# Linear-attention sums taken per head from projected values, and one more band of filter taps on TensorE

## The chip, the cores and the metric

The kernel runs on one core of one Trainium2 chip. The metric is the device time of one execution in microseconds (us). Three runs of the kernel before gave a median of 3430.04 us (3429.32 to 3433.61). One further execution was recorded by the hardware profiler.

Engines are named as in the profile: PE is TensorE's matrix multiplication and PEld its weight loads, DVE is VectorE, ACT is ScalarE, POOL is GpSimd, SP is the engine that issues most DMAs.

## What is computed

The input is x of 8 images, 384 channels, 64 x 64 pixels (4096 tokens each), in float32. Two residual layers follow one another, each on a group-normalised input:

```
# layer 0: linear attention, 6 heads of 64 channels
q = elu(rope(Wq x + bq) / 8) + 1
k = elu(rope(Wk x + bk)) + 1
v = Wv x + bv
kv    = einsum('bhnd,bhne->bhde', k, v)       # sum over 4096 tokens
k_sum = k.sum(tokens)
out   = einsum('bhnd,bhde->bhne', q, kv) / (q . k_sum + 1e-6)
x = x + Wfc out + bfc
# layer 1: 1x1 conv, FFT filter on 8x8 blocks, 3x3 depthwise conv, gate
t = irfft2(rfft2(blocks(w_in x)) * fft_filter)
t = depthwise_conv3x3(t, w_dw)                # 9 taps per channel
x = x + w_out (gelu(t[:192]) * t[192:])
```

## The kernel before

**Tiling.** The 384 channels are three tiles of 128 partitions. The 4096 tokens of an image are eight bands of 512 (8 rows of 64 pixels). `nb` is 8 images, `b` counts images, `j` bands, `m` and `t` channel tiles, `i` the four groups of 128 tokens in a band.

**Stages.** After a start-up that forms the keys of image 0, two stages alternate for each image.

- The *attention stage* of image b (`queries`, L823): per band a query projection (`q_project`, L527, PSUM tiles pq), rotation and elu on DVE and ACT, a normaliser (`q_normalise`, L565, pn, and `q_spread`, L589, prb), the output projection (`project_out`, L606, pf), which adds into x. Its end holds the norm chain of layer 1, a row of small dependent steps on PE, DVE and ACT. The key projections of bands 0 and 1 of the next image are put between these steps as filling.
- The *filter stage* of image b (layer 1): per band `expand_filter` (L624 pi, L638 pd, product tf on DVE at L646), `back_transform` (L659 pb, copied by ACT into one of two ring buffers, L669 to L675), `first_taps` (ACT) and `taps` (DVE, L720, eight scalar_tensor_tensor per channel tile), the gate (L726 to L731), and `contract` (L747 and L758, pw). The keys of image b+1 are formed here as well: an iterator `fill` is advanced between the pieces of each band.

**Keys and values before.** For all images, a band's keys are projected with tokens on the partitions (`k_project`, L432, pk; the bias is added by DVE at L435 into kc; the rotation is L415, L423, L439, the elu L337 to L339). The x of the same band is transposed by PE in twelve 128 x 128 pieces (`turn_tokens`, L398, px) and copied by ACT (L399) into xk, with a column of ones from POOL (L391). Then `kx_accumulate` (L447) sums keys times x, not keys times values: for each of the four token groups three matmuls of 128 key channels by 385 columns, into three PSUM banks `acc` that are held from band 0 of the filter stage to the end of the key sums. At j = 0 and 1 `fill` is the accumulation of bands 0 and 1. At j = 2 it is the projection of band 2, and from j = 3 on the projection of band j and the accumulation of band j-1.

`kv_finish` (L457) turns these sums into what the attention needs. It copies acc to kx (ACT L464, DVE L462), turns the key sums into a row (L468 pr), transposes kx (nine pieces, L485 pt, copied at L486), multiplies by the value weights per head (L494 pv, 24 matmuls of 64 columns in halves of the array and their bias row), copies the result into kvt_bd (DVE L502) and multiplies by wfc (L509 pm) into mt. Twelve POOL copies (L476) spread the key sums into ks_bd, which pn reads. The first three parts of `kv_finish` alternate with the three column blocks of `q_project(b, 1)`.

**Order.** Each engine works through a fixed order made when the program is built. It follows the program text, except that an instruction whose inputs are not due yet is passed by later ones. PSUM is eight banks, one tile each, that rotate; a matmul waits until a bank has been read out. `work` has nine slots for large SBUF tiles (tag w).

At the start of each attention stage three things of the filter stage are still open: the contraction of band 6 (`before_last`, called after `q_project(b, 0)`), the taps and gate of band 7 (`gate`, called in the loop at j = 0, 24 instructions of L720), and the contraction of band 7 (`output`, called at j = 2).

In the last image there are no next keys. Its filter stage runs `expand_filter`, `back_transform`, `first_taps`, `contract` and `taps` band by band. In bands 6 and 7 the third channel tile's nine taps are matmuls with diagonal matrices instead (`array_taps`, L694, ptap): `on_array` says which. In band 6 six of the nine are issued by `first_taps(b, 6)` and three by `taps(b, 6)`, since the last row comes from band 7.

Of the kernel before, what the change touches and what calls it, by code (L numbers as in the profile page):

```python
# [16 lines left out]
CT = 3  # L17
# [100 lines left out]
def conv_blocks_kernel(ctx: ExitStack, tc: tile.TileContext, a: dict, out: bass.AP, nb: int):  # L118
# [253 lines left out]
    def v_bias(b, params):  # L372

        p_ = ps_tile(f"pbv_{b}")
        nc.tensor.matmul(p_[:1, :C], params[2], group_w["wv"], start=True, stop=True)
        t = small.tile([1, C], F32, tag="krest", name=f"vbias_{b}", bufs=1)
        nc.vector.tensor_add(t, p_[:1, :C], bv)
        return t


    transposed = {}
# [19 lines left out]
    def k_project(b, j, wks, bias, kf):  # L401

        tk = qp.tile([P, 2, 4, 2, QC], F32, tag="turn", name=f"tk_{b}_{j}")
        nc.sync.dma_start(tk, a["tk"][:, j])
        xk = transposed.pop((b, j), None)
        early = xk is not None
        if not early:
            xk = xk_tile(b, j)
        kc = w_tile([P, 4, C], f"kc_{b}_{j}")
        ks = w_tile([P, 4, C], f"ks_{b}_{j}")  # L410
        def turn_keys(r):

            k, to = (t[:, r].rearrange("p i (g c) -> p (i g) c", g=2) for t in (kc, ks))
            cos, sin = (tk[:, i, r].rearrange("p i g f -> p (i g) f") for i in range(2))
            nc.vector.tensor_mul(  # L415
                to.rearrange("p g (s f two) -> p g s f two", s=2, two=2),
                k.rearrange("p g (s c) -> p g s c", s=2)[:, :, ::-1, :].rearrange(
                    "p g s (f two) -> p g s f two", two=2
                ),
                sin.rearrange("p g (s f) -> p g s f", s=2).unsqueeze(4).to_broadcast([P, 4, 2, QC // 2, 2]),  # L420
            )
            pairs = k.rearrange("p g (f two) -> p g f two", two=2)
            nc.vector.tensor_mul(pairs, pairs, cos.unsqueeze(3).to_broadcast([P, 4, QC, 2]))  # L423

        for i in range(4):

            def tokens(t):
                return xt[b, j][:, t, i * P : (i + 1) * P]

            pk = ps_tile(f"pk_{b}_{j}_{i}")  # L430
            for t in range(CT):
                nc.tensor.matmul(pk[:, :C], tokens(t), wks[:, t, :], start=(t == 0), stop=(t == CT - 1))  # L432
            if not early:
                turn_tokens(b, j, i, xk)
            nc.vector.tensor_add(kc[:, i, :], pk[:, :C], bias)  # L435
            if i % 2:
                turn_keys(slice(i - 1, i + 1))
            yield
        nc.vector.tensor_add(kc, kc, ks)  # L439
        elu_plus_one(kc, ks)  # L440
        kf[j] = kc, xk

    def kx_accumulate(b, j, kf, xk, acc):

        for i in range(4):
            for m in range(CT):
                nc.tensor.matmul(  # L447
                    acc[m][:, : C + 1],
                    kf[:, i, m * P : (m + 1) * P],
                    xk[:, i, :],  # L450
                    start=(j == 0 and i == 0),
                    stop=(j == NBAND - 1 and i == 3),
                )
            yield

    def kv_finish(b, acc, params, vb, wv, wfc, done):

        rs = params[0]
        kx = w_tile([P, CT, C + 1], f"kx_{b}")
        for m in range(CT):  # L460
            if m == 1:
                nc.vector.tensor_copy(kx[:, m, :], acc[m][:, : C + 1])  # L462
            else:
                nc.scalar.copy(kx[:, m, :], acc[m][:, : C + 1])  # L464
        row = small.tile([1, C], F32, tag="ksrow", name=f"ksrow_{b}", bufs=1)
        pr = ps_tile(f"pr_{b}")
        for m in range(CT):
            nc.tensor.matmul(  # L468
                pr[:1, m * P : (m + 1) * P], kx[:, m, C : C + 1], ident, start=True, stop=True
            )  # L470
        nc.scalar.copy(row, pr[:1, :C])
        for c0, at, n in QRUNS:

            for s in range(0, n, 32):
                h, c, q = (c0 + s) // HD, c0 + s, at + s
                nc.gpsimd.tensor_copy(  # L476
                    ks_bd[q % P : q % P + 32, q // P, h : h + 2 * NH + 1 : NH],
                    kx[c % P : c % P + 32, c // P, C : C + 1].to_broadcast([32, 3]),
                )
        yield  # L480
        xks = w_tile([P, CT, C], f"xks_{b}")
        for t in range(CT):
# [7 lines left out]
        for m in range(CT):  # L490
            for t in range(-1, CT):
                for h in range(2):
                    head = slice(m * P + h * HD, m * P + (h + 1) * HD)
                    nc.tensor.matmul(  # L494
                        pv[halves[h], m * HD : (m + 1) * HD],
                        vb[:, head] if t < 0 else wv[:, t, head],
                        row[:, head] if t < 0 else xks[:, t, head],
                        start=(t < 0),
                        stop=(t == CT - 1),
                    )  # L500
# [2 lines left out]
                kvt_bd[halves[h], :, halves[h]], pv[halves[h], :C // 2].rearrange("p (m k) -> p m k", m=CT)  # L503
            )
        yield
        mt = small.tile([P, CT, C], F32, tag="mt", name=f"mt_{b}", bufs=1)
        for t in range(CT):
            pm = ps_tile(f"pm_{b}_{t}")
            nc.tensor.matmul(pm[:, :C], kvt_bd[:, t, :], wfc[:, t, :], start=True, stop=True)  # L509
            for i, (c, at, n) in enumerate(QPIECES):  # L510
                if c // P == t:
                    dst, src = mt[at % P : at % P + n, at // P, :], pm[c % P : c % P + n, :C]
                    if i % 2:
                        nc.vector.tensor_copy(dst, src)
                    else:
                        nc.scalar.copy(dst, src)
        done.append(mt)


    def q_project(b, j, wqs, bias, q):  # L520
# [159 lines left out]

    def on_array(b, j):

        return b == nb - 1 and j >= NBAND - 2

    def make_diagonals():
        t = small.tile([P, CT, C], F32, tag="wk", name="diagonals", bufs=1).rearrange("p t c -> p (t c)")
# [24 lines left out]
    def taps(b, j):  # L711

        t, acc = ring[j % 2], dw[b, j]
        if on_array(b, j) and j < NBAND - 1:
            array_taps(b, j, range(6, 9))
        for m in range(CT - on_array(b, j)):
            for k in range(1, 9):
                src = t[:, m, k // 3 : k // 3 + 8, k % 3 : k % 3 + W]
                wd = w_dw[:, m, k : k + 1]
                nc.vector.scalar_tensor_tensor(acc[:, m], src, wd, acc[:, m], ALU.mult, ALU.add)  # L720
# [84 lines left out]
    class Keys:  # L805
# [5 lines left out]
                self.params, self.wk, self.bias = prepared  # L811
                self.kf = {}

        def project(self, j):
            if self.live and j < NBAND:
                yield from k_project(self.b, j, self.wk, self.bias, self.kf)

        def accumulate(self, j):
            if self.live and 0 <= j < NBAND:
                if j == 0:  # L820
                    self.acc = [ps_tile(f"acc_{self.b}_{m}") for m in range(CT)]
                yield from kx_accumulate(self.b, j, *self.kf.pop(j), self.acc)

        def prepare(self, j):

# [4 lines left out]
                scale_weight(self.wq, self.params, scale)  # L830
                self.qbias = q_bias(self.b, self.params)
            if self.live and j == NBAND:
                self.wv, self.wfc = (load_weight(self.b, n, k_runs) for n in ("wv", "wfc"))
                if self.b == 0:
                    sum_weight(self.wv, "wv")
                self.vbias = v_bias(self.b, self.params)

    def queries(b, keys, before_last, gate, output):


        params, wq, qbias, wv, wfc, vbias = keys.params, keys.wq, keys.qbias, keys.wv, keys.wfc, keys.vbias
        q, done = {}, []
        run(q_project(b, 0, wq, qbias, q))
        before_last()
        run(keys.accumulate(NBAND - 1))
        finish = kv_finish(b, keys.acc, params, vbias, wv, wfc, done)
        for _ in zip(q_project(b, 1, wq, qbias, q), finish):
            pass
        prepared = []
# [44 lines left out]
    keys = Keys(0, prepared)  # L894
    run(keys.project(0))

    bv = const_tile([1, C], "bv", a["bv"].unsqueeze(0), nc.sync)
    bq = const.tile([P, CT], F32, tag="bq", name="bq")
    for c0, at, n in QRUNS:

# [47 lines left out]
    for b in range(nb):  # L948
        prepared = queries(b, keys, before_last, gate, output)
        keys = Keys(b + 1, prepared)  # L950
        params = []
        chain, more = norm_chain(b, 1, params), chain_of(keys.project(0), keys.project(1))
        last = b == nb - 1
        if last:

# [7 lines left out]
        run(more)  # L963
        if last:
            break
        first_sums = chain_of(keys.accumulate(0), keys.accumulate(1))
        for j in range(NBAND):
            fill = chain_of(keys.project(j), keys.accumulate(j - 1 if j > 2 else NBAND)) if j > 1 else first_sums
            tf = []
            h = normalised(b, j, params, (8, 8), "f") if j else ahead  # L970
            store_x(b, j)
            if 1 <= j < NBAND - 1:
                load_x(b + 1, j + 1)
            layer1 = expand_filter(b, j, h, tf)
            next(layer1)
            next(fill)
            run(layer1)
            next(fill)
            next(fill)
            back_transform(b, j, tf[0])  # L980
            first_taps(b, j)
            next(fill)
            if j > 1:
                contract(b, j - 2)
            if j > 0:
                run(fill)
            keys.prepare(j)
            if j > 0:
                depthwise_gate(b, j - 1)
            stream_stats(b + 2, j)  # L990
# [15 lines left out]
    for j in range(NBAND):  # L1006
# [4 lines left out]
        if j < NBAND - 1:  # L1011
            h = normalised(b, j + 1, params, (8, 8), "f")
        back_transform(b, j, tf[0])
        first_taps(b, j)
        if j >= 2:
            contract(b, j - 2)
# [48 lines left out]
```

## Time and profile before

| | us |
|---|---|
| median of 3 runs | 3430.04 |
| the profiled execution | 3431.62 |
| its span, first to last instruction | 3428.8 |
| granted TensorE clock, mean | 0.994 |
| filter stage of image 1 (751.3 to 988.0) | 236.7 |
| attention stage of image 2 (988.0 to 1170.8) | 182.8 |
| filter stage of image 7 (3249.7 to 3428.8) | 179.1 |

A stage is counted here from the first record of pq (L527) or of pi (L624) of an image. The stages of images 1 to 5 repeat to 0.1 us. Between the profiled span and the execution's own time lie 2.8 us.

How to read it: a row of groups ends with busy time and mean duration of one, then the idle time of its engine before it and what ended that. A matmul in float32 here has two records; a transpose has one. Records overlap, since the array is a pipeline: what one more costs is the distance between starts, not the duration of one.

### The profile page before, as it was taken

How to read it: one execution, taken by the hardware profiler on the slowest of the kernel's cores; microseconds unless marked ns; L12 is line 12 of the kernel's file. 1: busy time of each engine (PE TensorE's matmuls, PEld its weight loads, DVE VectorE, ACT ScalarE, POOL GpSimd, SP SyncE). 2: the span in 40 equal slices, each digit the busy share in tenths (PEclk: the TensorE clock that was granted, in tenths of full speed). 3: DMA queues.
4: the chain of work that ended last, by engine and by line, in shares of the span. 5: the costliest groups of instructions: out<-in, count | busy, mean ns of one | idle time of the engine just before them, and what ended most of it. 6: DMA issues, size and time to landing. Idle time of an engine off the chain costs nothing.

```text
span 3428.8 us, 50015 instructions
## 1 busy us (share of the span) xinstructions
PE 3337.2 (97%) x19760; PEld 1866.2 (54%) x19760; DVE 2801.2 (82%) x4396; ACT 1958.6 (57%) x3869; POOL 140.2 (4%) x247
## 2 busy tenths in 40 slices
PE   8999999999999999999999999999999999999988
PEld 5545555455654556545565455654556445564454
DVE  6586888869898698986989869897698967989598
ACT  4445666456655567545665557555576455554553
POOL 0000001000010000100001000010000000000000
PEclk9999999999999999999999999999999999999999
DMA  6323234333243333442343423334243331333113
GB/s 219 113 90 108 70 107 97 124 118 80 78 108 122 109 84 88 106 127 93 84 105 99 126 93 93 100 97 124 84 111 89 102 121 47 83 85 96 61 25 51
DMA packets 149328, 335.60 MB, mean 98 GB/s; under 512 B 27125, under 2 KB 38246, under 8 KB 140902
## 3 DMA queue, kind: packets, MB, share of 16 engines
q1 hardware_dynamic: 123702, 282.65, 24.8%
q0 software_dynamic: 25200, 49.55, 9.2%
q8 instruction: 155, 2.54, 0.3%
q14 instruction: 79, 0.65, 0.1%
q10 hardware_dynamic: 192, 0.21, 0.0%
HBM read 232.51 MB, written 99.88 MB: 97 GB/s over the span
## 4 chain that ended last, share of the span: by engine, by line
PE 64%; DVE 28%; ACT 5%; issue 2%; DMA 0%; SPq 0%; DVEq 0%; ACTq 0%
DVE dw L720 17%; PE pf L606 15%; PE pq L527 13%; PE acc L447 10%; PE pk L432 8%; PE pi L624 6%; PE pw L747 3%; PE pb L659 2%; DVE kc L439 2%; PE pd L638 2%; PE pw L758 1%; DVE kc L339 1%; DVE kc L435 1%; ACT ring L669 1%; PE pn L565 1%
## 5 line engine op out<-in xcount | busy, mean ns | idle before, releaser
L720 DVE SCALAR_TENSOR_TENSOR dw<-ring,w_dw,dw 128x512 f32<-128x512 f32 x1520 | 1061.4, 744 | 179.3 <-ACT ring L675 137.7
L432 PE MATMUL pk<-wk,x 128*128 128x384 f32 x1536 | 547.2, 495 | 8.7 <-DVE kc L435 8.7
L527 PE MATMUL pq<-x,wq 128*128 128x512 f32 x1152 | 520.8, 599 | 4.0 <-ACT qs L554 3.9
L606 PE MATMUL pf<-qc,mt 128*128 128x512 f32 x1152 | 513.6, 599 | 0.0
L624 PE MATMUL pi<-w_in,hf 128*128 128x384 f32 x1536 | 510.8, 489 | 2.1 <-ACT hf L332 1.3
L447 PE MATMUL acc<-xk,kc 128*128 128x385 f32 x1488 | 504.0, 492 | 0.0
L624 PEld LDWEIGHTS pi<-w_in,hf 128*128 128x128 f32 x1536 | 290.4, 191 | 204.9 <-issue 5.1
L447 PEld LDWEIGHTS acc<-xk,kc 128*128 128x128 f32 x1488 | 276.4, 190 | 204.5 <-issue 22.8
L432 PEld LDWEIGHTS pk<-wk,x 128*128 128x128 f32 x1536 | 278.1, 190 | 197.5 <-issue 22.8
L527 PEld LDWEIGHTS pq<-x,wq 128*128 128x128 f32 x1152 | 211.9, 190 | 255.1 <-issue 240.7
L606 PEld LDWEIGHTS pf<-qc,mt 128*128 128x128 f32 x1152 | 213.0, 190 | 250.0 <-issue 232.8
L399 ACT COPY xk<-px 128x384 f32<-128x384 f32 x248 | 118.1, 486 | 324.5 <-PE px L398 324.5
L631 ACT COPY ht<-pi 128x384 f32<-128x384 f32 x256 | 120.2, 479 | 235.7 <-PE pi L624 235.1
L610 DVE SCALAR_TENSOR_TENSOR x<-pf,bfc,x 128x512 f32<-128x512 f32 x192 | 140.9, 742 | 106.8 <-PE pf L606 106.2
L435 DVE TENSOR_TENSOR kc<-pk,kbias 128x384 f32<-128x384 f32 x256 | 141.2, 552 | 86.9 <-PE pk L432 85.6
L747 PE MATMUL pw<-gated,w_out 128*128 128x256 f32 x768 | 183.9, 386 | 5.7 <-DVE kc L435 5.6
L337 ACT ACTIVATE qs<-qc 128x1536 f32<-128x1536 f32 x64 | 95.0, 1484 | 158.0 <-DVE qc L556 148.0
L554 ACT ACTIVATE qs<-pq,qbias 64x512 f32<-64x512 f32 x128 | 87.3, 682 | 168.1 <-DVE qc L540 167.2
L179 ACT ACTIVATE differences<-x,shift 128x512 f32<-128x512 f32 x168 | 119.9, 714 | 77.1 <-DVE x L610 77.1
L777 POOL DMA_DIRECT2D out_dram<-y x63 | 80.7, 1281 | 2019.2 <-ACT y L772 1938.7
L669 ACT COPY ring<-pb 128x256 f32<-128x256 f32 x384 | 115.8, 406 | 81.3 <-PE pb L659 81.3
L747 PEld LDWEIGHTS pw<-gated,w_out 128*128 128x128 f32 x768 | 141.8, 192 | 33.6 <-DVE kc L435 11.3
(157 smaller groups left out, 4354.3 us busy)
## 6 DMA issues: line engine op xcount, KB each, us to landing
tq<-in_tq SPq DMA_DIRECT2D x64, 1024.0 KB, 4.8
x<-in_x SPq DMA_DIRECT2D x64, 768.0 KB, 6.3
tk<-in_tk SPq DMA_DIRECT2D x64, 768.0 KB, 4.5
out_dram<-x SPq DMA_DIRECT2D x63, 768.0 KB, 3.3
out_dram<-y POOLq DMA_DIRECT2D x63, 768.0 KB, 7.9
xs<-in_x SPq DMA_DIRECT2D x56, 768.0 KB, 5.8
wk<-in_wk SPq DMA_DIRECT2D x8, 576.0 KB, 3.9
wv<-in_wv SPq DMA_DIRECT2D x8, 576.0 KB, 3.7
```

The costliest lines, as they stand in the source:

```text
L179: nc.scalar.activation(out[:, m, :], x_[:, m, :], AF.Identity, bias=shift[:, m : m + 1], accum_out=of_m[0])
L432: nc.tensor.matmul(pk[:, :C], tokens(t), wks[:, t, :], start=(t == 0), stop=(t == CT - 1))
L435: nc.vector.tensor_add(kc[:, i, :], pk[:, :C], bias)
L447: nc.tensor.matmul(acc[m][:, : C + 1], kf[:, i, m * P : (m + 1) * P], xk[:, i, :], start=(j == 0 and i == 0), stop=(j == NBAND - 1 and i = ...
L527: nc.tensor.matmul(p_, wqs[:, t, m * P : (m + 1) * P], xt[b, j][:, t, :], start=(t == 0), stop=(t == CT - 1),)
L606: nc.tensor.matmul(p_, mt[:, t, m * P : (m + 1) * P], q[:, t, :], start=(t == 0), stop=(t == CT - 1))
L610: nc.vector.scalar_tensor_tensor(xm, p_, bfc[:, m : m + 1], xm, ALU.add, ALU.add)
L624: nc.tensor.matmul(p_[:, :C], h[:, t, i * P : (i + 1) * P], w_in[:, t, :], start=(t == 0), stop=(t == CT - 1),)
L631: nc.scalar.copy(ht[:, i, :], p_[:, :C])
L669: nc.scalar.copy(rows[:, u], ps[u][:, m - m0].rearrange("p s i (r c) -> p r s i c", r=8))
L720: nc.vector.scalar_tensor_tensor(acc[:, m], src, wd, acc[:, m], ALU.mult, ALU.add)
L747: nc.tensor.matmul(p_[h][:, m - m0, :], w_out[:, 0, m * P : (m + 1) * P], gated[:, h * HT : (h + 1) * HT], start=(m == m0), stop=False,)
```

## The change

For image 0 nothing changes but names. For images 1 to 7:

- The transposes of x (px) and their copies go. `v_project` projects the values with tokens on the partitions (twelve matmuls of 384 columns a band), and ACT copies them into a tile with 65 columns a head, the last one ones.
- `kv_accumulate` multiplies keys by values per head: 24 matmuls a band, 64 key channels by 65 columns, even heads into the upper and odd heads into the lower half of one PSUM bank.
- `kv_finish_heads` replaces `kv_finish`: one copy, six small DVE instructions that add the value bias times the key sums, three transposes.
- The value weights are loaded and scaled with the next image's keys (`load_values`), into the buffer of mt.
- `fill` has more pieces: the values of band 0 and 1 now come in the filter stage at j = 0 and 1, those of later bands after each piece of keys.

In the last image the third tile's taps of band 3 go to TensorE too, and the last three of a band's matmuls are issued ahead of the next `first_taps`.

```diff
     def k_project(b, j, wks, bias, kf):
...
-        early = xk is not None
-        if not early:
+        early = b or xk is not None
+        if b:
+            xk = w_tile([P, 4, NH, HD + 1], f"v_{b}_{j}")
+            nc.gpsimd.memset(xk[:, :, :, HD:], 1.0)
+        elif not early:
             xk = xk_tile(b, j)
...
+    def v_project(b, j, wvs, v):
+        for i in range(4):
+            pv = ps_tile(f"pv_{b}_{j}_{i}")
+            for t in range(CT):
+                nc.tensor.matmul(pv[:, :C], xt[b, j][:, t, i * P : (i + 1) * P], wvs[:, t, :],
+                    start=(t == 0), stop=(t == CT - 1))
+            nc.scalar.copy(v[:, i, :, :HD], pv[:, :C].rearrange("p (h d) -> p h d", h=NH))
+            yield
+
+    def kv_accumulate(b, j, kf, v, acc):
+        for i in range(4):
+            for head in range(NH):
+                m, h = head // 2, head % 2
+                nc.tensor.matmul(
+                    acc[halves[h], m * (HD + 1) : (m + 1) * (HD + 1)],
+                    kf[:, i, head * HD : (head + 1) * HD],
+                    v[:, i, head, :],
+                    start=(j == 0 and i == 0 and m == 0),
+                    stop=(j == NBAND - 1 and i == 3 and m == CT - 1))
+            yield
...
+    def kv_finish_heads(b, acc, vb, wfc, done):
+        kx = w_tile([P, CT, HD + 1], f"kx_{b}")
+        nc.scalar.copy(kx, acc[:, : CT * (HD + 1)].rearrange("p (m d) -> p m d", m=CT))
+        key_sums(kx, HD)
+        for m in range(CT):
+            for h in range(2):
+                head = 2 * m + h
+                nc.vector.scalar_tensor_tensor(kvt_bd[halves[h], m, halves[h]],
+                    vb[halves[h], head * HD : (head + 1) * HD], kx[halves[h], m, HD : HD + 1],
+                    kx[halves[h], m, :HD], ALU.mult, ALU.add)
+        yield
+        kvt = w_tile([P, CT, P], f"kvt_{b}")
+        pt = ps_tile(f"pt_{b}")
+        for m in range(CT):
+            nc.tensor.transpose(pt[:, m * P : (m + 1) * P], kvt_bd[:, m, :], ident)
+        nc.scalar.copy(kvt, pt[:, : CT * P].rearrange("p (m k) -> p m k", m=CT))
+        yield
+        yield
+        fold(b, kvt, wfc, done)
...
-        return b == nb - 1 and j >= NBAND - 2
+        return b == nb - 1 and j in (3, NBAND - 2, NBAND - 1)
...
-        if on_array(b, j) and j < NBAND - 1:
-            array_taps(b, j, range(6, 9))
...
+        def load_values(self):
+            if self.live:
+                self.wv = small.tile([P, CT, C], F32, tag="mt", name=f"wv_{self.b}", bufs=1)
+                nc.sync.dma_start(self.wv, w_in_dram["wv"])
+                scale_weight(self.wv, self.params)
+            yield from ()
...
-        chain, more = norm_chain(b, 1, params), chain_of(keys.project(0), keys.project(1))
+        chain, more = norm_chain(b, 1, params), chain_of(keys.project_k(0), keys.load_values(), keys.project_k(1))
...
-        first_sums = chain_of(keys.accumulate(0), keys.accumulate(1))
+        first_values = keys.project_v(0)
+        next(first_values, None)
         for j in range(NBAND):
-            fill = chain_of(keys.project(j), keys.accumulate(j - 1 if j > 2 else NBAND)) if j > 1 else first_sums
+            if j < 2:
+                fill = chain_of(keys.project_v(j) if j else first_values, keys.accumulate(j))
+            else:
+                fill = chain_of(keys.project(j), keys.accumulate(j - 1 if j > 2 else NBAND))
...
         back_transform(b, j, tf[0])
+        if j and on_array(b, j - 1):
+            array_taps(b, j - 1, range(6, 9))
         first_taps(b, j)
```

`fold` and `key_sums` are the old ends of `kv_finish` under names of their own. The value bias becomes a tile of 128 equal rows.

## The prediction

> **What bounds the kernel now.** I read the page's busy shares first, then the groups by form, then a table of stretches through one round of stages (filter stage of image 1, attention stage of image 2), then PE's and DVE's timelines where that table shows DVE full.
>
> ```profile
> PE 3337.2 (97%) x19760; PEld 1866.2 (54%) x19760; DVE 2801.2 (82%) x4396; ACT 1958.6 (57%) x3869; POOL 140.2 (4%) x247
> ...
> 751.30:789.30 38.00, 37.95 (x321) 22.06 (x322) 23.73 (x36) 21.83 (x47) 0.37 (x2) 1.00 0.33 104
> 789.30:816.10 26.80, 25.04 (x198) 15.62 (x196) 26.12 (x42) 17.28 (x39) 0.00 (x0) 1.00 0.11 31
> 816.10:852.50 36.40, 33.61 (x223) 20.49 (x222) 36.16 (x52) 29.21 (x57) 2.79 (x4) 1.00 0.50 132
> ...
> 974.70:1019.90 45.20, 45.20 (x201) 25.69 (x199) 42.75 (x65) 27.62 (x46) 8.39 (x14) 1.00 0.45 103
> 1019.90:1071.60 51.70, 51.14 (x268) 24.93 (x265) 47.81 (x79) 25.27 (x42) 0.00 (x0) 1.00 0.32 111
> 1071.60:1149.50 77.90, 77.90 (x334) 34.69 (x333) 54.51 (x93) 43.66 (x96) 1.48 (x3) 1.00 0.39 119
> ```
>
> The columns after the length are PE, PEld, DVE, ACT, POOL, then clock and DMA. PE is full nearly everywhere, so PE work is the first price. But DVE is full too in two places: bands 2 and 3 of the filter stage (26.12 of 26.8, 36.16 of 36.4), where PE stalls, and the stretch from 974.7, when the ring of band 7 is ready, to 1071.6, the end of the contraction of band 7 (90.6 of 96.9).
>
> **PE's work per image.** Starts, not durations, are the price.
>
> ```profile
> L432 PE MATMUL pk<-wk,x 128*128 128x384 f32 x1536 | 547.2, 495 | 8.7 <-DVE kc L435 8.7
> L447 PE MATMUL acc<-xk,kc 128*128 128x385 f32 x1488 | 504.0, 492 | 0.0
> L398 PE MATMUL px<-groups,x 128*128 128x128 f32 x768 | 124.4, 277 | 12.1 <-DMA x<-in_x 6.5 <-ACT ht L631 4.7 <-ACT ring L399 0.4
> L494 PE MATMUL pv<-xks,wv 128*64 128x64 f32 x288 | 13.6, 230 | 0.0
> ```
>
> ```profile
> 1007.87 2.74 PE L527 MATMUL pq<-x,wq 128*128 128x512 f32 x6
> 1010.54 0.82 PE L468 MATMUL pr<-groups,kx 128*1 128x128 f32 x6
> 1011.29 2.84 PE L527 MATMUL pq<-x,wq 128*128 128x512 f32 x6
> 1013.97 1.15 PE L485 MATMUL pt<-groups,kx 128*128 128x128 f32 x9
> 1014.96 2.74 PE L527 MATMUL pq<-x,wq 128*128 128x512 f32 x6
> 1017.63 0.33 PE L494 MATMUL pv<-ksrow,vbias 1*64 1x64 f32 x4
> 1017.89 0.57 PE L494 MATMUL pv<-xks,wv 128*64 128x64 f32 x12
> ```
>
> Median distances of starts in the trace: pk 322 ns, acc 323, px 109 (pt too: 0.99 us for nine above).
> - Removed: px 96 x 0.109 = 10.5 us; acc 192 x 0.323 = 62.0; in the finish pr 0.75, pt 0.99, pv 2.27 (1017.63 to pn at 1019.90) = 4.0. Sum 76.5.
> - Added: values 192 records x 0.322 = 61.9; three transposes 0.33. The per-head sums have the form of pv but 65 columns for 64. There two records, one per half, start 7 ns apart and the next two 52 ns later (single records): 58.5 ns for two. A band has 24 such twos, 1.40 us; change of form costs about 0.15 (100 for 52 ns at the second two, 152 for 52 on leaving). 1.55 x 8 = 12.4. From below, the two halves could not beat 52 ns a two (-0.16 us a band); from above, each two at the 100 ns that follows a change of form is +1.0 us a band. I take the row. Sum 74.6.
>
> Net -1.9 us. It is moved as well: the filter stage loses px of six bands (7.85) and seven acc bands (54.3) and gains 31 of 32 value groups (60.0) and seven sums (10.9): **+8.7 us**. The attention stage loses px of two bands (2.6), one acc band (7.75), the finish (4.0) and gains 1.94 + 1.55 + 0.33: **-10.6 us**.
>
> The Trainium skill, "TensorE: Matmul & The Clock Gate", section on PE-mode transpose, gives about 275 ns for one in a kernel. The mean duration here agrees, 277 ns. Priced so, px would be worth 26.4 us an image and the change over 110 us more; the starts 109 ns apart decide. "TensorEngine Tiling (Array Packing)", Key Properties, says that a change of tiling mode drains the array, which speaks against sums in half-array form; the row shows some 0.1 us, and the four pieces of a band run in one block, so it is paid once a band.
>
> **The filter stage.** Single starts that come late by over 0.3 us add to 6.7 us in image 1, nearly all put down to DVE's kc (L435): PE waits for banks while DVE is full. Work ahead of band 3 grows: band 0 by -0.4, band 1 by +1.6, band 2 by +6.4 (values for px, no sums in either). That is 7.6 us more time for the same DVE work, and two more banks rotate. So the stalls are filled rather than added to: I leave 1.0 of 6.7 (ends 0 and 5). Stage: +8.7 - 5.7 = **+3.0 us**. Value copies replace px copies on ACT (L399, 486 ns); ACT is 156 of 237 us busy there.
>
> **The attention stage.** Here the cover is thin. From 974.7 to 1071.6 PE's 96.9 us become 96.9 + 1.6 (values for the last px) - 6.2 - 6.2 - 3.7 = 82.4. DVE's 90.6 stay: two copies go (L462, L502: 0.55 + 0.72), six instructions on 64 x 64 come (0.15 to 0.34 each, ends from a 3-column operation, 162 ns, and L579, 345 ns). 17.6 us of them are taps and gate of band 7 (24 x 0.663 + 1.7). Before, they run between 989 and 1013 in the gaps of the query work, long before they are wanted at 1067; after, PE comes 14.5 us earlier and the gaps shrink. DVE becomes the bound, and PE waits for banks.
> - From below: DVE without any idle has done by 1065.3 what it had done at 1070.2 (4.9 us idle there); PE may lead by 5.4 us (the end of contract to pn at 1077, which needs DVE's last q). PE at 1059.9 where its own work ends at 1057.1: 2.8 us lost.
> - From above: some 13 taps are still open when `gate` stands first in order; q3 (3 banks), prb (4) and one pf fill all eight, and pn waits till the taps are done: 8 to 9 us, plus 2 for ks_bd below, up to 13.
> - I take **6.5**: in the last tile's chain of taps the trace shows other instructions in every second place (1009 to 1013), so q3's reads come before the chunk ends.
>
> POOL's twelve copies (6.35 us, at 1008.0) stand behind ACT's kx copy, which stands behind the elu of q0 (1007.49) and behind POOL's issue of band 6's output (1.28). PE comes to pn 8.1 us after the sums instead of 12; a wait of 0 to 2.5 us, counted in the 6.5.
>
> The norm chain loses 0.33 us of cover at each step: at ps_r, rsg is ready 0.9 us early now and three px lie before it. 0.4 us (0 to 1.5). The weights wv are loaded when the last pf frees mt (1149.7) and wanted after some 17 us; such a load takes 3.7 us, scaling 3 x 0.41 on a DVE that is 14.45 of 21.3 us busy. On SP only tk of band 1 is queued behind it. Nothing, unless the order puts scaling ahead of keys: then at most 4 us of DVE's slack of 6.9.
> Stage: -10.6 + 6.5 + 0.4 = **-3.7 us**.
>
> **Last image.** Bands 2 to 5 of 18 to 21 us have DVE at 19.9 of 20 us. Eight taps fewer save 8 x 0.663 = 5.3; PE gets 18 records of 429 ns = 7.7 us in a band with some 4 idle, after a wait of 1.7 for the ring as in band 6. Ends 0 and -5.3; I take -4, nearer DVE, since its queue holds a band of taps meanwhile. Moving three taps of band 6 earlier: 0 (at most 1 either way).
>
> **Sum.** 7 x (3.0 - 3.7) - 4 = -8.9 us on 3431.6: 3422.7. That execution stands 1.6 above the median: **3421**.
>
> **Rivals.**
> - A, forecast: Q loss 4.5 to 8.5 us an image: 7 x (-2.7 to +1.3) - 4: 3407 to 3435. Chance 0.40.
> - B, DVE keeps up better and stalls vanish: loss 2.8 to 4.5: 3388 to 3407. For: filler order left 4.9 us idle. 0.17.
> - C, slower: bank wait at pn of band 2, as above. It decides from a loss of 7.8 us, where an image's round breaks even with the -4; at 8.5 to 13: 3435 to 3467. For: DVE 93% full in that stretch. Against: order may favour query work. 0.26.
> - D: the head sums at 100 ns a two: +1.0 x 56 = 56 us, 3477. Against: pv's row. 0.09.
> - E: DVE is no bound at all (loss 0): 7 x (-7.2) - 4 = -54, 3376. 0.08.
>
> Range 3388 to 3464 leaves out D and most of E; A's own range is 3407 to 3435. A measurement here can tell 0.2%, so faster is under 3423.2, slower above 3436.9: faster is 0.23 of A's 0.40 with B and E, 0.48; same the rest of A and the edge of C, 0.19; slower C and D, 0.33.
>
> **What would show it.** Filter stage near 239.7 us with few waits for kc L435; attention stage near 179; in its first 80 us DVE at 95% or more and PE waiting at pn or pf for DVE taps; head sums 58 to 60 ns a two; image 7's filter stage near 175. Wrong if PE shows no wait there (E), or if the order on DVE lets band 7's taps block the queries (C).

## The result and the profile after

The changed kernel takes 3444.21 us (median of 5 runs, 3441.70 to 3445.18) beside 3431.76 us for the kernel before on the same chip. The ratio is 1.0036, interval 1.0023 to 1.0049: **slower by some 12 us**, where 9 us faster was forecast. The profiled execution took 3442.33 us, its span 3440.6 us (before 3428.8).

The span, cut at the first record of pq and of pi of each image (all in us):

| stage | before | after | difference | predicted |
|---|---|---|---|---|
| start-up and first attention stage | 331.9 | 332.0 | +0.1 | 0 |
| filter stages of images 0 to 6, sum | 1654.5 | 1646.4 | -8.1 | +21.0 |
| attention stages of images 1 to 7, sum | 1263.3 | 1272.2 | +8.9 | -25.9 |
| filter stage of image 7 | 179.1 | 190.0 | **+10.9** | -4.0 |

So the seven rounds of the values part come out at +0.8 us, from two errors of opposite sign, and nearly all of the loss stands in one stage of one image: the last filter stage, where a band's taps moved to TensorE. Lines of the changed kernel: pk L438, values pv L454, head sums acc L470 (image 0 keeps its own at L483), pq L597, pn L635, pf L676, pi L694, pd L708, tf L716, pb L729, the ring copies L739 to L745, ptap L764, taps on DVE L788, gate L794 to L799, pw L815 and L826.

The page's busy shares, after:

```profile
PE 3319.7 (96%) x21374; PEld 1856.2 (54%) x21374; DVE 2786.9 (81%) x4430; ACT 1976.0 (57%) x3854; POOL 143.2 (4%) x247
```

PE is busy 17.5 us less and DVE 14.3 us less, and the span is 11.8 us longer. Less work on both engines with a longer span means waits, and the next table says where they are. It has bands 0 and 1, 2, and 3 of the filter stage of image 1, then three stretches of the attention stage of image 2 (length; PE, PEld, DVE, ACT and POOL busy; clock; DMA):

```profile
751.70:790.40 38.70, 38.70 (x400) 23.23 (x398) 22.47 (x36) 23.71 (x52) 0.41 (x2) 1.00 0.32 103
790.40:823.20 32.80, 31.66 (x223) 19.13 (x221) 27.33 (x44) 19.93 (x46) 0.00 (x0) 1.00 0.08 25
823.20:855.70 32.50, 32.50 (x259) 20.32 (x257) 29.65 (x44) 23.05 (x48) 1.44 (x2) 1.00 0.42 104
979.70:1011.10 31.40, 29.85 (x188) 17.09 (x187) 31.16 (x46) 21.00 (x30) 7.77 (x13) 1.00 0.61 137
1011.10:1072.90 61.80, 53.38 (x265) 25.55 (x265) 59.24 (x102) 29.71 (x45) 0.63 (x1) 0.97 0.28 98
1072.90:1150.00 77.10, 77.10 (x333) 34.33 (x332) 54.52 (x93) 43.33 (x95) 1.55 (x3) 1.00 0.40 121
```

In the filter stage DVE has idle time now (27.33 of 32.8, 29.65 of 32.5; it was full in both bands before) and PE is full. In the attention stage the roles are exchanged: up to 1072.9 DVE is 90.40 of 93.2 us busy and PE 83.23, so PE waits some 10 us there. What it waits for, from the waits of PE in that whole stage (total, times, longest):

```profile
PE pn L635 <- DVE qc L339: 5.7, 3, 3.4
PE pf L676 <- DVE qs L610: 2.9, 2, 1.8
PE pn L635 <- DVE qs L610: 0.6, 1, 0.6
```

The groups by form, after:

```profile
L438 PE MATMUL pk<-wk,x 128*128 128x384 f32 x1536 | 545.0, 496 | 0.0
...
L676 PE MATMUL pf<-qc,mt 128*128 128x512 f32 x1152 | 518.8, 604 | 17.1 <-DVE qs L610 17.0
...
L454 PE MATMUL pv<-wv,x 128*128 128x384 f32 x1344 | 470.0, 488 | 0.0
...
L708 PE MATMUL pd<-ht,dft 64*64 64x384 f32 x1024 | 97.3, 495 | 0.0
L470 PE MATMUL acc<-v,kc 128*64 128x65 f32 x2688 | 92.2, 224 | 6.9 <-ACT v L461 6.9
L635 PE MATMUL pn<-qc,ks_bd 128*32 128x128 f32 x1536 | 56.4, 277 | 44.8 <-DVE qc L339 36.1 <-DVE qs L610 7.9 <-POOL ks_bd L498 0.8
```

Beside them, a group of the same view before that the prediction did not show:

```profile
L638 PE MATMUL pd<-ht,dft 64*64 64x384 f32 x1024 | 119.4, 500 | 12.1 <-DVE kc L435 11.9 <-ACT ht L631 0.2
```

The idle time that DVE's kc ended before keys (8.7 us) and before pd (11.9 of 12.1) is 0.0 now. The busy time of pd fell as well, from 119.4 to 97.3 us for the same 1024 records: the records are hardly shorter (500 and 495 ns on average), they overlap more. A start that comes late by less than the duration of the record before it shows as busy time, not as idle time. The new prices are 6.9 us over the whole run before acc, for ACT's copies of the values, and the queries' waits for DVE: 44.8 us before pn and 17.1 before pf, where before both rows had 0.0:

```profile
L606 PE MATMUL pf<-qc,mt 128*128 128x512 f32 x1152 | 513.6, 599 | 0.0
...
L565 PE MATMUL pn<-qc,ks_bd 128*32 128x128 f32 x1536 | 55.2, 277 | 0.0
```

The timeline of PE in band 3 of the last image (start, us, instruction, idle before it):

```profile
3296.70 8.01 PE L694 MATMUL pi<-w_in,hf 128*128 128x384 f32 x24
3304.64 1.52 PE L708 MATMUL pd<-ht,dft 64*64 64x384 f32 x16
3309.74 1.85 PE L729 MATMUL pb<-idft,tf 64*64 64x64 f32 x48 [3.58 <-DVE tf L716]
3312.16 1.56 PE L729 MATMUL pb<-idft,tf 64*64 64x64 f32 x48 [0.57 <-DVE tf L716]
3315.64 7.81 PE L764 MATMUL ptap<-ring,diagonals 128*128 128x512 f32 x12 [1.91 <-ACT ring L744]
3323.28 2.75 PE L815 MATMUL pw<-gated,w_out 128*128 128x256 f32 x12
```

The idle time that I meant to fill, 3.58 us, is still there, untouched, ahead of pb. The taps stand behind pb, after a new wait of 1.91 for the ring. They run for 7.81 us, with nothing of the band beside them. The band takes 30.8 us where it took 20.9: 1.91 + 7.81 = 9.7 of the 9.9 more.

### The profile page after: what moved, and what is told of

The parts are those of the page before. It is cut to its first block, busy times and chain, and to the rows that moved or that the text cites. A ratio compares the mean times of both kernels' runs of the same rounds, so it can differ in the third digit from the quotient of the medians.

```text
span 3440.6 us, 53200 instructions
## 1 busy us (share of the span) xinstructions
PE 3319.7 (96%) x21374; PEld 1856.2 (54%) x21374; DVE 2786.9 (81%) x4430; ACT 1976.0 (57%) x3854; POOL 143.2 (4%) x247
## 4 chain that ended last, share of the span: by engine, by line
PE 76%; DVE 18%; ACT 4%; issue 1%; DMA 0%; SPq 0%; DVEq 0%; ACTq 0%
PE pi L694 14%; PE pk L438 13%; PE pf L676 13%; PE pv L454 12%; PE pq L597 7%; DVE dw L788 6%; PE pw L815 4%; PE pd L708 2%; PE pb L729 2%; PE pw L826 2%; PE acc L483 2%; PE acc L470 2%; DVE qc L339 1%; DVE qc L610 1%; ACT ring L739 1%
## 5 line engine op out<-in xcount | busy, mean ns | idle before, releaser
L788 DVE SCALAR_TENSOR_TENSOR dw<-ring,w_dw,dw 128x512 f32<-128x512 f32 x1512 | 1059.5, 749 | 262.5 <-ACT ring L745 223.9
L438 PE MATMUL pk<-wk,x 128*128 128x384 f32 x1536 | 545.0, 496 | 0.0
L676 PE MATMUL pf<-qc,mt 128*128 128x512 f32 x1152 | 518.8, 604 | 17.1 <-DVE qs L610 17.0
L597 PE MATMUL pq<-x,wq 128*128 128x512 f32 x1152 | 528.1, 607 | 0.1
L694 PE MATMUL pi<-w_in,hf 128*128 128x384 f32 x1536 | 516.1, 492 | 1.3 <-ACT hf L332 1.3
L454 PE MATMUL pv<-wv,x 128*128 128x384 f32 x1344 | 470.0, 488 | 0.0
L438 PEld LDWEIGHTS pk<-wk,x 128*128 128x128 f32 x1536 | 283.5, 191 | 205.3 <-issue 32.5
L694 PEld LDWEIGHTS pi<-w_in,hf 128*128 128x128 f32 x1536 | 287.8, 191 | 196.3 <-issue 4.6
L676 PEld LDWEIGHTS pf<-qc,mt 128*128 128x128 f32 x1152 | 214.8, 191 | 271.3 <-issue 231.8
L597 PEld LDWEIGHTS pq<-x,wq 128*128 128x128 f32 x1152 | 215.2, 193 | 255.8 <-issue 244.4
L454 PEld LDWEIGHTS pv<-wv,x 128*128 128x128 f32 x1344 | 253.6, 190 | 181.4 <-issue 8.4
L461 ACT COPY v<-pv 128x384 f32<-128x384 f32 x224 | 108.8, 486 | 417.8 <-PE pv L454 417.1
L815 PE MATMUL pw<-gated,w_out 128*128 128x256 f32 x768 | 177.5, 380 | 0.2 <-DVE gated L795 0.2
L337 ACT ACTIVATE qs<-qc 128x1536 f32<-128x1536 f32 x64 | 95.1, 1486 | 135.9 <-DVE qc L626 125.8
L815 PEld LDWEIGHTS pw<-gated,w_out 128*128 128x128 f32 x768 | 145.0, 190 | 34.7 <-issue 5.7
L337 ACT ACTIVATE ks<-kc 128x1536 f32<-128x1536 f32 x64 | 95.2, 1487 | 100.9 <-DVE kc L445 72.0
```

Source lines behind the costliest of these rows:

```text
L337: nc.scalar.activation(e, x_, AF.Relu, scale=-1.0)
L454: nc.tensor.matmul(pv[:, :C], xt[b, j][:, t, i * P : (i + 1) * P], wvs[:, t, :], start=(t == 0), stop=(t == CT - 1),)
L597: nc.tensor.matmul(p_, wqs[:, t, m * P : (m + 1) * P], xt[b, j][:, t, :], start=(t == 0), stop=(t == CT - 1),)
L676: nc.tensor.matmul(p_, mt[:, t, m * P : (m + 1) * P], q[:, t, :], start=(t == 0), stop=(t == CT - 1))
L694: nc.tensor.matmul(p_[:, :C], h[:, t, i * P : (i + 1) * P], w_in[:, t, :], start=(t == 0), stop=(t == CT - 1),)
L815: nc.tensor.matmul(p_[h][:, m - m0, :], w_out[:, 0, m * P : (m + 1) * P], gated[:, h * HT : (h + 1) * HT], start=(m == m0), stop=False,)
```

## The experiments

Two theories to begin with. **T (taps):** the last image loses the time, because the matmuls of band 3 stand on PE's path and what DVE saves doesn't come back. **Q (queries, the prediction's rival C):** the values part makes DVE the bound of the attention stage, and that is what is lost. Stage lengths are from each kernel's profiled execution, and ratios are against runs of the kernel before beside it.

**The two parts, each alone.** The first takes band 3 back to DVE:

```diff
     def on_array(b, j):
-        return b == nb - 1 and j in (3, NBAND - 2, NBAND - 1)
+        return b == nb - 1 and j >= NBAND - 2
```

> The changed kernel with band 3 of the last image back on DVE (on_array holds for bands 6 and 7 alone). Theory 'last image' (the loss is band 3's matmuls): the last filter stage falls from 190.0 to 179 to 181 us, the time from 3444 to 3433 to 3435, which is 1 to 3 us above before. Rival 'attention stage' (the loss is the wait for DVE there and band 3 gains the 4 us forecast): the time rises to about 3448. Both: the attention stages stay at 184.3, the filter stages of images 0 to 5 at 235.4.

Measured: 3432.84 us, ratio 1.0004 (0.9995 to 1.0014). Image 7's filter stage 180.9 us, the other stages as in the changed kernel (235.4 and 184.3).

The second puts the taps part into the kernel before:

```diff
     def on_array(b, j):
-        return b == nb - 1 and j >= NBAND - 2
+        return b == nb - 1 and j in (3, NBAND - 2, NBAND - 1)
...
-        if on_array(b, j) and j < NBAND - 1:
-            array_taps(b, j, range(6, 9))
...
+        if j and on_array(b, j - 1):
+            array_taps(b, j - 1, range(6, 9))
```

> The kernel before with the taps part alone: band 3's third tile on TensorE, the last three matmuls of a band ahead of the next first_taps. Theory 'last image': the last filter stage goes from 179.1 to about 190, the time from 3431.8 to 3442 to 3443. Rival 'attention stage': the last filter stage falls by 4 to 175, the time to 3428.

Measured: 3443.16 us, ratio 1.0033 (1.0021 to 1.0046); image 7's filter stage 191.5, band 3 30.5. The taps part carries the whole loss, with or without the new values. T holds for the total. The first kernel is still 1.8 us above before in the last filter stage; it differs there by the place of the last three matmuls of band 6. The values part with those put back is the next kernel (the second hunk above, reversed):

> The values part alone: the changed kernel with band 3's taps back on DVE and the last three matmuls of band 6 back in their old place. Theory: the rounds of images 1 to 7 are worth +1.3 us in all and moving the three matmuls costs 1.8 of the 2.0 us that the values-only kernel lost in image 7, so image 7's filter stage is 179.1 us again, the profiled span about 3430 and the ratio 1.000 (0.999 to 1.001). If it is still 181, the place of the three matmuls was not the cause.

Measured: 3430.43 us, ratio 1.0000 (0.9992 to 1.0009), span 3428.0, image 7's filter stage 179.1 as before. So the values part is worth nothing, and moving the three matmuls, costed at 0 +/- 1, costs 1.8 us (1.6 by the medians, each against its own before). Ahead of band 7's taps, these six records stand in one block of 24 at a point where the contractions of the last bands are still to come. Most of the 1.8 us lies behind PE's last matmul: from its end to the end of the span it is 9.67 us with the new place and 8.19 with the old. In the profiled executions of all kernels it is 9.1 to 9.9 us with the new place and 8.1 to 8.3 with the old. What lengthens that end was not tested.

**Where band 3's ten microseconds come from.** Behind the taps waits the contraction of band 1, and ACT's gate of the next band needs the tile that it frees. So the taps may cost more by what they delay than by themselves. First, the six matmuls behind that contraction (the changed kernel otherwise; `first_array_taps` is the two lines of `first_taps` that issue them):

```diff
-        if on_array(b, j):
+        if on_array(b, j) and j != 3:
             first_array_taps(b, j)
...
         if j >= 2:
             contract(b, j - 2)
+        if j == 3:
+            first_array_taps(b, j)
```

> The changed kernel with band 3's first six matmuls put behind the contraction of band 1 instead of ahead of it. If the delay of that contraction is the cost (ACT waits 9.0 us for it before it may write gated, DVE's chain then waits 2.0), the last filter stage falls from 190 to 183 to 185 and the time to about 3438. If PE's own 7.7 us in a place without idle is the cost, it stays at 188 to 190 and the time at 3442 to 3444.

Measured: 3440.14 us, ratio 1.0026 (1.0015 to 1.0037), image 7's filter stage 188.3. The stage is 1.7 us shorter than in the changed kernel; by the medians the loss against before falls by 3.6 us, from 12.5 to 8.9. Not all of that is the contraction: the twelve records take 5.42 us here instead of 7.81, and while band 3 becomes 4.6 us shorter (26.2), bands 4 and 5 become 3.6 longer. The delayed contraction is not the main cost, and its own share is not separated.

Then the matmuls where PE really waits, between the forward and the backward transform of band 4:

```diff
         layer1 = expand_filter(b, j, h, tf)
         run(layer1)
+        if j == 4:
+            first_array_taps(b, 3)
...
         back_transform(b, j, tf[0])
```

> The changed kernel with band 3's first six matmuls put between the forward transform and the back transform of band 4, where PE waits 2 to 4 us for DVE's tf anyway. If the place is the cost, the matmuls take PE's idle time, DVE keeps its saving of 5.3 us, and the last filter stage falls from 190 to 176 to 179, the time to 3430 to 3433. If matmuls in that stage cost as such (a lower granted clock, 637 ns each), it stays above 185 and the time above 3439.

Measured: 3436.89 us, ratio 1.0017 (1.0007 to 1.0026), image 7's filter stage 184.6. The timeline of PE in band 4 of this kernel:

```profile
3325.10 1.52 PE L708 MATMUL pd<-ht,dft 64*64 64x384 f32 x16
3326.55 5.42 PE L764 MATMUL ptap<-ring,diagonals 128*128 128x512 f32 x12
3331.90 1.63 PE L729 MATMUL pb<-idft,tf 64*64 64x64 f32 x96
```

The wait for tf is gone, and the same twelve records take 5.42 us instead of 7.81: half of the loss came from the place. The kernel is still slower than with the taps on DVE. PE has 5.42 + 2.84 us more to do in band 4, and waits 0.41 us for the ring before the last three taps; the wait that they cover is 2.5 us. That would be +6.2, and the stage is 3.7 us longer than in the values-only kernel (184.6 beside 180.9). So by this estimate only some 2.5 us came back from DVE, not 5.3. This run leaves the DVE work out alone:

```diff
-        for m in range(CT - on_array(b, j)):
+        for m in range(CT - (on_array(b, j) or (b == nb - 1 and j == 3))):
             for k in range(1, 9):
```

> The values part alone, and in the last image eight DVE taps of the third tile of band 3 are left out and nothing takes their place (part of the depthwise convolution of that band is missing). It shows by itself what 5.3 us less of DVE work is worth there. The prediction's own pricing: DVE bounds bands 2 to 5, image 7's filter stage falls by 4 to 5.3 us against the values part alone. Rival: PE's own loop of 18.3 us a band stands just below DVE's 20, so only 1.5 to 3 us come back.

Measured: 3428.31 us, ratio 0.9993 (0.9984 to 1.0002) to before; image 7's filter stage 176.4, 2.7 us below the values part alone (2.1 by the medians). 5.3 us of DVE work taken out, at no cost to anyone, is worth 2.7 us at most, and almost none of it in the bands where DVE is full: bands 3, 4 and 5 take 21.0, 19.7 and 19.8 us beside 20.8, 19.7 and 20.2, band 6 24.9 beside 27.7. DVE's timeline in band 4 of this kernel says why:

```profile
3316.91 6.71 DVE L790 SCALAR_TENSOR_TENSOR dw<-ring,w_dw,dw 128x512 f32<-128x512 f32 x10
3323.53 0.69 DVE L797 TENSOR_TENSOR gated<-gated,dw 128x512 f32<-128x512 f32 x1
3324.13 3.40 DVE L790 SCALAR_TENSOR_TENSOR dw<-ring,w_dw,dw 128x512 f32<-128x512 f32 x5
3327.56 0.42 DVE L801 TENSOR_TENSOR gated<-gelu,dw 64x256 f32<-64x256 f32 x1
3328.01 0.42 DVE L801 TENSOR_TENSOR gated<-gated,dw 64x256 f32<-64x256 f32 x1
3328.47 1.95 DVE L716 TENSOR_TENSOR tf<-pd,filt 128x384 f32<-128x384 f32 x4
3330.34 7.37 DVE L790 SCALAR_TENSOR_TENSOR dw<-ring,w_dw,dw 128x512 f32<-128x512 f32 x11
```

PE's pd of this band is done near 3326.7, and it waits for tf, which stands in DVE's order behind fifteen taps. Eight taps fewer don't shorten that: in the values part alone the same fifteen stand ahead of tf, DVE stays full in both, and PE still waits 2.33 us for tf in this band (2.5 us in the values part alone). What is saved shows in band 6, and there much of it is TensorE's clock. These are the first twelve records of band 6's own matmul taps, which both kernels have, in the values part alone and then with the eight taps left out:

```profile
3371.39 7.33 PE L764 MATMUL ptap<-ring,diagonals 128*128 128x512 f32 x12 [1.68 <-ACT ring L744]
```

```profile
3372.28 5.42 PE L764 MATMUL ptap<-ring,diagonals 128*128 128x512 f32 x12 [1.77 <-ACT ring L744]
```

These 1.9 us are most of band 6's 2.8. The wait for tf ahead of them is 2.28 us in the first kernel and 1.65 in the second. But kernels that leave nothing out in this image have 5.42 us here as well (the one with `gate` at j = 1 and the one with six taps on TensorE, both below). So the 5.3 us are worth some 0.8 us without the clock and 2.7 with it; whether the missing taps cause the faster clock is not shown.

**The attention stage.** Is DVE the bound there, as Q says, and was PE before? Both kernels with eight DVE taps of band 7 left out in images 0 to 6, the first on the values-only kernel, the second on the kernel before:

```diff
-        for m in range(CT - on_array(b, j)):
+        for m in range(CT - (on_array(b, j) or (b < nb - 1 and j == NBAND - 1))):
             for k in range(1, 9):
```

> The values part alone (band 3 on DVE), and the eight DVE taps of the third channel tile left out in band 7 of images 0 to 6, 5.3 us of DVE work in the crowded start of each attention stage. This leaves out part of the depthwise convolution. If DVE's work there is the bound, the attention stages of images 1 to 6 fall from 184.3 to 178.5 to 180 and the time from 3432.8 to about 3400. If PE waits for the length of the chains there (key sums through POOL, the elu), they stay at 183 to 184.3.

Measured: 3399.44 us, ratio 0.9907 (0.9887 to 0.9927). The stage falls from 184.3 to 179.4 us (180.1 in image 2): 4.9 of the 5.3 us that DVE lost. One wait does not move, though. In image 2 the waits of pf and pn for qs (2.9 and 0.6 us in the changed kernel) are gone, and the waits of pn for qc are still there:

```profile
PE pn L635 <- DVE qc L339: 4.2, 2, 3.4
```

The longest of them is 3.35 us, to the digit as in the changed kernel. This is what stands ahead of it on ACT, two passes of the elu (L337, L338) with a table load between them:

```profile
1014.68 1.49 ACT L337 ACTIVATE qs<-qc 128x1536 f32<-128x1536 f32 x1 [1.37 <-DVE qc L626]
1016.19 1.28 ACT L338 ACT_TABLE_LOAD   x1
1017.48 1.48 ACT L338 ACTIVATE qs<-qs 128x1536 f32<-128x1536 f32 x1
```

DVE's last step of the elu (L339, 1.76 us) starts at 1019.00, right behind it, and pn at 1020.90. So this wait is the length of the elu's chain through DVE and ACT, with PE out of work that could stand beside it; fewer taps on DVE don't shorten it. In images 4 and 6 it is there as well (3.3 us), and the waits for qs fall only from 3.6 to 2.1 us. Most of the gain there is PE's busy time, 172.3 us beside 175.6 in the values part alone, at a granted clock of 1.00 beside 0.98: fewer waits, and a clock that stays up.

> The kernel before with the same eight taps left out in band 7 of images 0 to 6. If PE is the bound of the attention stage there, it stays at 182.8 (by 0.5 at most) and the time at 3428 to 3431. If DVE bounded it before already, the stage falls by 3 to 5.

Measured: 3426.56 us, ratio 0.9987 (0.9977 to 0.9998); the stage falls by 0.5, from 182.8 to 182.3. The same cut is worth 33 us (3432.84 - 3399.44) in the one kernel and 4.5 in the other. Q's mechanism is real: the change took PE's bound off this stage, and DVE's work counts there now (together with the elu's chain, which PE's longer work covered before). It is just not what made the total slower, since the filter stage gave the time back.

If only the order of DVE's work were the trouble, starting the taps of band 7 later would free the queries. The values-only kernel with `gate` at j = 1 and the contraction of band 7 at j = 3:

```diff
-            if j == 0:
+            if j == 1:
                 gate()
...
-            if j == 2 and b < nb - 1:
+            if j == 3 and b < nb - 1:
                 output()
```

> The values part alone, with the taps and gate of band 7 called one band later in the attention stage (j = 1) and the contraction of band 7 at j = 3. If the place of the 24 taps in DVE's order is what makes PE wait, the stage falls from 184.3 to 179 to 181 and the time from 3432.8 to 3405 to 3420. If only the sum of DVE's work counts, the wait moves along with the taps and the stage stays within 1 us.

Measured: 3451.72 us, ratio 1.0061 (1.0044 to 1.0077), attention stages 186 to 187.5 us: longer, outside both expectations. One step later still, and with the last three matmuls of band 6 in their old place:

> The same with the gate at j = 2 and the contraction at j = 4, and the last three array taps of band 6 back in taps, as before the change. The old place is worth 1.8 us in the last filter stage (180.9 to 179.1). If spreading DVE's 17.6 us over more bands of PE work helps, the attention stage falls to 175 to 179 and the time to 3385 to 3410; if not, it stays at 184.

Measured: 3440.38 us, ratio 1.0027 (1.0018 to 1.0036); its runs spread from 3434.61 to 3446.96. Within the profiled execution the stage takes 184.1 to 187.0 us, with the same instructions in each of the images 1 to 6. The waits of PE in the attention stage of image 6, first with `gate` at j = 1, then at j = 2:

```profile
PE ps_m L273 <- DVE mv L204: 4.6, 1, 4.6
PE pn L635 <- DVE qc L339: 4.3, 2, 3.3
```

```profile
PE pn L635 <- DVE qc L339: 6.6, 3, 3.3
PE pf L676 <- DVE qs L610: 1.7, 1, 1.7
PE ps_r L281 <- DVE rsg L310: 1.2, 1, 1.2
```

In the values part alone, PE waits 4.3 us for qc here (longest 3.3), 2.8 at pf and 0.8 at pn for qs. With `gate` later the waits for qs fall by 2.5 and 1.9 us, and the longest wait stays at 3.3. More is added elsewhere: in the norm chain of the next image (ps_m waits 4.6 us for DVE's mean), or at pn for qc (6.6) and at ps_r. The spread of the last kernel goes with TensorE's granted clock: its mean is 0.989 to 0.990 in the three runs up to 3434.98 us and 0.986 in the three from 3444.44 us on. In the profiled execution the two long stages (187.0 and 185.7 us) have two stretches of 3.4 us at a granted clock of 0.50, the other four have one. What decides on the second is not shown.

What helps is less DVE work in that stretch, put on PE exactly where PE waits:

```diff
+        def carry(b=b):
+            j = NBAND - 1
+            dw_pe[b, j] = ps_tile(f"ptap_{b}_{j}")
+            array_taps(b, j, range(6), 5)
+            nc.scalar.copy(dw[b, j][:, 2].rearrange("p r w -> p (r w)"), dw_pe.pop((b, j)))
...
         if j == 0:
             run(finish)
             mt = done[0]
+            carry()
```

`array_taps` is given the last of its taps (here 5) for `stop`. ACT forms the diagonals once an image in the buffer of wk, which is free at that time, and `taps` begins at tap 6 for this tile. The same with all nine taps:

> The values part alone, and in images 0 to 6 all nine taps of the third tile of band 7 are matmuls, put just ahead of the normaliser of band 1, where PE waits up to 3.4 us for DVE; ACT copies the sum out, and ACT forms the diagonals once an image. DVE loses 8 x 0.663 = 5.3 us of its burst, PE gets 18 x 0.429 = 7.7 us in a stretch where it waits about 10. If DVE is the bound of the attention stage after the change, the stage falls from 184.3 to 181 to 183 us and the kernel to some 3408 to 3423 us. If PE's own work is (almost) the bound again, it rises by 3 to 5 us an image, to over 3450.

> As the kernel with nine taps of band 7 as matmuls, but six on TensorE (5.1 us) and three left on DVE, which loses 5 x 0.663 = 3.3 us. If the stage is set by a balance of the two engines, this is within 1 us an image of the kernel with nine: attention stage 181 to 183 us. If DVE alone sets it, the stage is 184.3 - 3.3 x 0.92 = 181.3, with the factor 4.9 of 5.3 from the run that left eight taps out, and nine would give 179.4.

Measured: nine 3413.83 us, ratio 0.9952 (0.9939 to 0.9964), stage 181.7; six **3411.68 us, ratio 0.9946 (0.9932 to 0.9960), stage 181.4**. Both are faster than before and after. Six falls where DVE alone would put it (181.3 was expected). Nine doesn't (179.4 by DVE alone): PE is busy 179.7 of its 181.7 us and is the bound again, beside 177.2 of 181.4 with six. The timeline of PE in image 2, first of the changed kernel, then of the one with six:

```profile
1019.97 2.10 PE L508 MATMUL pm<-wfc,kvt 128*128 128x384 f32 x6
1025.41 0.86 PE L635 MATMUL pn<-qc,ks_bd 128*32 128x128 f32 x24 [3.35 <-DVE qc L339]
1026.21 0.35 PE L659 MATMUL prb<-parts,expand 32*128 32x128 bf16 x12
1026.48 9.69 PE L597 MATMUL pq<-x,wq 128*128 128x512 f32 x18
```

```profile
1015.34 2.10 PE L508 MATMUL pm<-wfc,kvt 128*128 128x384 f32 x6
1017.28 5.31 PE L767 MATMUL ptap<-ring,diagonals 128*128 128x512 f32 x12
1022.52 0.86 PE L635 MATMUL pn<-qc,ks_bd 128*32 128x128 f32 x24
1023.32 0.35 PE L659 MATMUL prb<-parts,expand 32*128 32x128 bf16 x12
1023.59 7.99 PE L597 MATMUL pq<-x,wq 128*128 128x512 f32 x18
```

Twelve records of taps stand where PE waited 3.35 us, and the query block behind them takes 7.99 us instead of 9.69, since PE had no pause ahead of it. In the kernel with six the granted clock is 1.00 in all its attention stages of images 1 to 6. So the gain has two sources, less work on DVE and a covered wait, and that 181.4 agrees with 181.3 does not show that DVE alone sets the stage.

## Why the prediction was wrong, point by point

- **Last image, the step that failed:** "PE gets 18 records of 429 ns = 7.7 us in a band with some 4 idle, after a wait of 1.7 for the ring as in band 6 ... I take -4, nearer DVE". It cost +10.9. Three things in it were wrong. The 4 us idle lie ahead of pb, and the taps need the ring, which needs pb: idle time that stands before an instruction's input can't hide it. The taps ran right behind those waits at a granted clock of 0.50 (3310.3 to 3320.4), twelve records in 7.81 us instead of 5.4. And the -5.3 of DVE is worth -2.7 at most by itself, since tf's place in DVE's order sets the band, not the sum of DVE's work. The upper end of 0 assumed that PE's part was covered; the uncovered price, 7.7 + 1.7 by the prediction's own numbers, was left out as an end.
- **Moving three taps of band 6:** 0, "at most 1 either way"; 1.8 us by two kernels that differ in nothing else.
- **PE's work per image:** the head sums were taken at 58.5 ns a two: the starts in the trace after are 7 and 52 ns apart, 59 a two, with 150 ns on leaving the form. Rival D falls. The busy time of PE in the filter stage of image 1 is 230.2 before and 234.2 after. That is +4.0, not the +8.7 of work, because groups that were stretched by waits shrank.
- **Filter stage:** +3.0 was forecast, -1.2 came. The waits were mis-sized: 6.7 us were single starts over 0.3 us late, and waits inside groups of pd, pb and pw added 4.4 (their busy time in that stage fell from 55.1 to 50.7). So +8.7 less 11.1, plus some 1 us of acc's wait for ACT, comes to about -1.4 beside the -1.2.
- **Attention stage:** -3.7 was forecast, +1.5 came (images 1 to 6). The term is the loss by DVE's burst, taken as 6.5 in bounds of 2.8 to 13: it was 11.7 (1.5 + 10.6 - 0.4). The named place was right (pn and pf waiting for DVE), the make-up only in part. Waits for banks behind the taps (pf and pn for qs) are 3.5 us in image 2. The larger part, 5.7 us, is pn waiting for qc itself, and its longest wait, 3.35 us, is the elu's chain, which no term had: it is there with eight taps fewer too. The half clock behind it adds 1.7 (9.69 for 7.99), which I had in no term either.
- **Rival C** had the bank waits, and its loss of about 12 us lies well past the 7.8 us from which it was to decide. But that point took the filter stage at +3.0 and the last image at -4; with -1.2 in the filter stage a round breaks even at a loss of 11.4 (1.2 + 10.6 - 0.4), and they nearly did. That 3444 us lies in C's 3435 to 3467 is luck: in C the rounds lose the time, here they lose 0.8 us and the last image the rest.
- **Sum:** the rounds missed by 5.7 us (+0.8 for -4.9), the last image by 14.9.

## What to carry to other kernels

Before work is moved onto an engine's idle time, ask where the inputs of that work are ready: idle time ahead of the instruction that feeds them hides nothing, and the price here was the full duration plus a new wait. What the relieved engine gives back is read from the place of its urgent instruction in its order, not from its busy share; leaving the work out once, in a run of its own, prices it. And when a change makes one engine lighter, the same stretch should be weighed again for the other: here the gain lay in six taps put exactly into the wait that the change had opened. That wait was a chain that the removed work had covered; ask of work that is to be taken away what it hides.

## What the runs showed of the hardware

- After PE had waited 3.6, 0.6 and 1.9 us within 9.5 us (3306.2 to 3315.6), the first distance between starts of taps was 1015 ns, the next four 853 to 854, then one of 641, then 429. Without a wait ahead, in the kernel with the taps in band 4, the first was 534 and the others 429. One wait of 3.35 us in the attention stage was enough for the same: four distances of 813 to 854 ns, and the next 18 query records took 9.69 us instead of 7.99. The granted clock of these two stretches, in the changed kernel:

```profile
3310.30:3320.40 10.10, 7.62 (x88) 4.64 (x89) 10.01 (x17) 4.74 (x12) 0.00 (x0) 0.50 0.01 2
1026.80:1030.10 3.30, 3.30 (x5) 1.25 (x4) 3.25 (x6) 1.42 (x4) 0.00 (x0) 0.50 0.00 0
```

- Shorter waits did it only sometimes. Behind the 2.33 us in band 4 of the kernel with band 3's eight taps left out the granted clock is 0.50 as well (3330.0 to 3333.3); behind a wait of 2.04 us in band 5 of the changed kernel (3358.2 to 3364.9) it stays at 1.00. So a wait can cost more than its length, and its cover can save more.
